# The last batch's attention ordered by query halves in a two-layer transformer kernel

## The chip, the cores and the metric

The kernel runs on one core of one Trainium2 chip. The metric is the device time of one execution in microseconds (us); every time below is in us unless it says ns. Engine names follow the profile: PE is the matmul engine and PEld its weight loads, DVE the vector engine, ACT the scalar (activation) engine, POOL the GpSimd engine, SP the sync engine, whose queue issues most of the DMAs.

## What is computed

Two transformer layers over a float32 tensor x of 4 batches, 1024 tokens each, 128 channels. Every sublayer is a layer norm with a per-batch scale and shift, the sublayer, and a gated addition to x. Cut to what matters here:

```python
# layer 0: causal attention, then a top-2 mixture of 8 experts (gelu)
# layer 1, attention
dense  = softmax(q @ k.T / sqrt(8)) @ v          # 16 heads of width 8
sparse = keep_top(softmax(Q @ K.T / 8), 204) ... @ V  # one head of width 64, renormalised
fused  = sig * (dense @ out_proj) + (1 - sig) * sparse
y = layernorm(h + fused) * g1 + b1
y = layernorm(y + relu(y @ ff1) @ ff2) * g2 + b2
x = x + gate * y
# layer 1, experts: top 2 of 8, at most 160 places for each expert and batch
h = layernorm(x) * (1 + cb) + sb
x = x + gate * (weighted sum of the two experts' relu MLPs)
```

## The kernel before

**Layout.** Tokens lie on the 128 partitions, 8 tiles of 128 tokens for each batch; "half h" means 4 tiles, or 512 tokens. The whole of x stays on the chip.

**Layer 1's attention loop.** The loop goes over units (batch b, head group g of 4 heads, query half h), 32 in all, and in each over 8 steps k (a tile of 128 keys). One step is written as two half-steps. A half-step computes scores for two heads (`weighed`: matmul `pw` from `kg` and `qa`, exponent `prT` on ACT), runs one piece of the row maxima for a later unit (`maxima`: two matmuls `pm` from `qg` and `kg`, one reduction `mxh` on DVE, twenty pieces ahead), and multiplies the previous step's exponents with the values (`values`: `pav`). At a unit's end its `pav` is copied to `raw`, transposed (`pr`) and divided into `cn` (`divided`). Before, a batch's units go through g, and for each g through both halves. `project(b, g)` loads q and k of a head group from DRAM (`qk`) by 8 DMAs on SP, into one of two `qg` and two `kg` buffers.

**Work beside the steps.** Everything else is written as generators (`Part`) that give up control after each piece and tell what it costs on P, A, D, G (PE, ACT, DVE, POOL). After each half-step, `between(n)` picks pieces whose due time has come, by a cost model of the four engines, which fixes the order in which each engine gets its instructions; each engine then runs its own list in order. A part has a first and a last step between which its work should be spread. The parts are:

- `begin(b)`: norm, q, k, v and the sparse head's projections of batch b
- `looked(b, four)`: the sparse attention of four query tiles; scores `pk`, exponents `exq`, a search for the threshold of the top 204 (ACT sign counts `junk`, DVE), exact selection (`lfq`, DVE), then `ended` for each tile: transposes `ptk` and the product `po` into `sp`
- `end(b)`: needs `cn` and `sp`; output projection (`ctxT`, `pdn`), norm l1, feed-forward in four blocks of 256 tokens (`ph`, `hid`, `pf`), norm l2, gated addition to x. Its additions and multiplications by rows run on POOL (`by_gpsimd`)
- `sends_of(b)`, through `sent_out`: norm f, transposes `ptf`, router (`pl`, `routed`, with the places `pp` from sums over all tokens before), and 16 indirect DMAs on POOL that scatter the tokens into the experts' places in DRAM (`sent`)

**The tail.** When the loop is over, its buffers are given up and `feed_forward` loads layer 1's expert weights (16 DMAs of 256 KB) into their room. `drain` then writes the rest, taking the first part in its list that the model says can start: the last batch's end and sends, `worked_on` for each batch in turn (per expert: `got` loaded, transposes `ptg`, `hs` on DVE, `ph`, `hid` on ACT, `py`, addition `y` on DVE, store to `done`), and `fetched` for each batch (16 indirect DMAs on POOL that gather `ys` from `done`, ACT and DVE work on them, and the store of the output). A batch's `worked_on` comes after the one before; the last batch's comes after its sends, and its gathers come last.

Layer 0 has the same parts at the start: two rounds of `worked_on`, the second of them beside the gathers of the first and the begin of layer 1's batch 0.

Of the kernel before, what the change touches and what calls it, by code (L numbers as in the profile page):

```python
# [15 lines left out]
P = 128  # L16
# [5 lines left out]
G = 4  # L22
# [21 lines left out]
TAX_A, TAX_D = (0.4, 3), (1.5, 2)  # L44
ROWS = ["out_b", "vp_b", "ff2_b", "ln1_g", "ln1_b", "ln2_g", "ln2_b"]
# [3 lines left out]
def kernel(ctx: ExitStack, tc: tile.TileContext, a: dict, out: bass.AP):  # L49
# [239 lines left out]
    def normalized(dst, src, name):  # L289

        n = src.shape[1]
        st = small.tile([P, n, 6], F32, tag="ln_st", name=f"st_{name}")
        mv = small.tile([P, n, 2], F32, tag="ln_mv", name=f"mv_{name}")
# [162 lines left out]
    def normal(dst, src, name):  # L456

        kind = name[:2].replace("0", "1")
        mv = small.tile([P, NT, 2], F32, tag=f"mv_{kind}", name=f"mv_{name}")
        bn = small.tile([P, NT, 6], F32, tag=f"st_{kind}", name=f"st_{name}")  # L460
        for i in range(NT):
            nc.vector.bn_stats(bn[:, i, :], src[:, i, :])
            if i % 4 == 3:
                yield "D!", ("D", 1.1)
        for i in range(NT):
            nc.vector.bn_aggr(mv[:, i, :], bn[:, i, :])
        rs = small.tile([P, NT], F32, tag=f"rs_{kind}", name=f"rs_{name}")
        nc.vector.tensor_scalar_add(rs, mv[:, :, 1], EPS)  # L468
        nc.gpsimd.tensor_tensor(rs, rs, mhalf, ALU.pow)  # L469
        yield "A", ("D", 1.4), ("G", 1.65)  # L470
        nb = small.tile([P, NT], F32, tag=f"nb_{kind}", name=f"nb_{name}")
        nc.vector.scalar_tensor_tensor(nb, mv[:, :, 0], -1.0, rs, ALU.mult, ALU.mult)
        for i in range(NT):
            nc.scalar.activation(
                dst[:, i, :], src[:, i, :], AF.Identity, bias=nb[:, i : i + 1],
                scale=rs[:, i : i + 1],
            )
            if i % 4 == 3:
                yield "A", ("D", 0.2 if i < 4 else 0.0), ("A", 1.15)

    def by_gpsimd(op, t, r):

        for h in range(NH):
            op(t[:, fours(h), :], t[:, fours(h), :], r(h))
# [19 lines left out]
    def routed(l, b, hT, wgt, wgtT, pool, ps, places=None):  # L504

        pl = ps.tile([P, NT, E], F32, tag="ms", name=f"pl{l}{b}")
        for i in range(NT):
            nc.tensor.matmul(
                pl[:, i, :], lhsT=hT[:, i * P : (i + 1) * P], rhs=router[l], start=True, stop=True
            )  # L510

        def new(tag, shape):
            return pool.tile(shape, F32, tag=tag, name=f"{tag}_{l}{b}")

        def wide(v):
            return v.unsqueeze(2).to_broadcast([P, NT, E])

        yield "D", ("P", 1.7)
# [13 lines left out]
        for i in range(NT):  # L532
            nc.vector.max(top[:, i, :], key[:, i, 0:E])
        yield "D", ("D", 1.5)
        nc.vector.memset(top[:, :, 2:8], KEY_PAD)
        left = new("r_left", [P, NT, 14])
        for i in range(NT):
            nc.vector.match_replace(left[:, i, :], top[:, i, :], key[:, i, :], KEY_CHOSEN)
        yield "D", ("D", 1.6)
# [16 lines left out]
        if l == 1 or places is not None:  # L556

            before = new("r_before", [P, NT, E])
            if l == 0 and b % 2:
                nc.vector.tensor_copy(before[:, 0, :], so_far[b - 1])  # L560
            else:
                nc.vector.memset(before[:, 0, :], 0.0)
            for i in range(1, NT):
                nc.vector.tensor_add(before[:, i, :], before[:, i - 1, :], chosen[:, i - 1, :])
            if l == 0 and b % 2 == 0:
                so_far[b] = new("r_so_far", [P, E])
                nc.vector.tensor_add(so_far[b], before[:, NT - 1, :], chosen[:, NT - 1, :])
            yield "", ("D", 1.4)
            pp = ps.tile([P, NT, E], F32, tag="ms", name=f"pp{b}")
# [8 lines left out]
        if places is not None:  # L578
# [5 lines left out]
                lg, pp, base[l].unsqueeze(1).to_broadcast([P, NT, E]), ALU.add  # L584
# [128 lines left out]
    def sent_out(l, b, xn, turn, fp):  # L713

        yield from normal(xn, x[:, b], f"f{l}")
# [9 lines left out]
        for h in range(NH):  # L725
# [11 lines left out]
            yield "!" if h == 0 else "", ("P", 1.1), ("A", 0.7)  # L737
        wgt = fp.tile([P, NT, E], F32, tag="wgt", name=f"wgt{l}{b}")
        into = fp.tile([P, NT, 2], mybir.dt.int32, tag="into", name=f"into{l}{b}", bufs=2)
        outof = const.tile([P, NT, 2], mybir.dt.int32, name=f"outof{l}{b}")  # L740
        both = const.tile([P, NT, 2], F32, name=f"both{l}{b}")
        yield from routed(l, b, hT, wgt, None, fp, ps, (into, outof, both))
# [3 lines left out]
        for i in range(NT):  # L746
# [14 lines left out]
        told[l, b] = outof, both  # L761

    def worked_on(l, q, w1, w2, b2r, act, fp):
# [63 lines left out]
        for i in range(len(units) + 2):  # L827
# [13 lines left out]
            if 1 <= i <= len(units):  # L841
                u = units[i - 1]
                for k0 in range(0, NK, 2):
                    up(u, k0)
                    us = u[2] * p / 512.0
                    yield "A!" if k0 == 0 else "!", ("P", 2.1 * us), ("A", 0.45 + 0.75 * us)
            if i >= 2:
                u = units[i - 2]
                down(u)
                yield "!", ("P", 1.07 * u[2]), ("D", 0.15 + 0.13 * u[2])  # L850
# [34 lines left out]
    def feed_forward(end, send):  # L885

        with tc.tile_pool(name="w1", bufs=1) as wpool, tc.tile_pool(name="f1", bufs=2) as fp:
# [11 lines left out]
            works[B - 1].after.append(send)  # L899
            drain([end, send, works[B - 1], gets[B - 1], *gets[:-1], *works[:-1]])  # L900
# [163 lines left out]
    def attention(general):  # L1064


        with tc.tile_pool(name=f"a1{general}", bufs=1) as ap, ExitStack() as wp_ctx:
# [19 lines left out]
            def turned(dst, src):  # L1087
                for h in range(NH):
# [4 lines left out]
                    yield "!" if h == 0 else "", ("P", 1.1), ("A", 0.6)  # L1093
# [3 lines left out]
            kgs = [ap.tile([P, T], F32, name=f"kg{i}") for i in range(2)]  # L1097
            for i in range(2):
                nc.gpsimd.memset(qgs[i], 0.0)
                nc.gpsimd.tensor_copy(kgs[i], ninth.to_broadcast([P, T]))  # L1100
# [26 lines left out]
            def project(b, g):  # L1127

                yield until(begins[b], "near", b)
                if g >= 2:  # L1130
                    assert ("qk", g - 1) in st[b]
                qg, kg = qgs[g % 2], kgs[g % 2]
                for s, to in ((1, kg), (0, qg)):
                    for j in range(4):
                        n = (4 * g + j) * DH
                        nc.sync.dma_start(
                            out=to[32 * j : 32 * j + DH, :], in_=qk[b][s, n : n + DH, :]
                        )
                st[b]["qk", g] = qg, kg
# [331 lines left out]
            def need(b, g):  # L1471

                if ("qk", g) not in st[b]:
                    projects[b, g].finish()
                return st[b]["qk", g]

            def shifted(b, g, h, mx):
# [5 lines left out]
                for q in range(4):  # L1483
# [5 lines left out]
                    qa, pt.rearrange("p q t -> p (q t)"), need(b, g)[0][:, half(h)], ALU.add  # L1489
# [4 lines left out]
            def maxima(b, g, h):  # L1494
# [3 lines left out]
                qg, kg = need(b, g)  # L1498
# [20 lines left out]
            def weighed(b, g, h, k, j):  # L1519
# [4 lines left out]
                    pw, lhsT=st[b]["qk", g][1][js, k * P : (k + 1) * P],  # L1524
# [4 lines left out]
            def values(b, g, h, k, part):  # L1529
# [20 lines left out]
                if (k, part) == (NT - 1, 1):  # L1550
                    raw = wp.tile([P, 512], F32, name="raw")
# [21 lines left out]
            def end(b):  # L1573
# [3 lines left out]
                by_gpsimd(nc.gpsimd.tensor_add, h_, lambda _: rows_of(o_b, 4))  # L1577
                by_gpsimd(nc.gpsimd.tensor_add, sp, lambda h: h_[:, fours(h), :])
                yield "!", ("G", 5.0)
                if b and not general:  # L1580
                    yield over(sends[b - 1])
                ctxT = ap.tile([P, T], F32, tag="x1T", name="ctxT")
                yield from turned(ctxT, cn)
                for h in range(NH):
# [9 lines left out]
                    yield "!" if h == 0 else "D", ("P", 1.1), ("D", 0.8)  # L1594
                x1 = h_
                yield from normal(x1, sp, f"l1{b}")
                for op, n in ((nc.gpsimd.tensor_mul, "ln1_g"), (nc.gpsimd.tensor_add, "ln1_b")):
                    by_gpsimd(op, x1, lambda _: rows_of(row[n], 4))
                    yield "", ("G", 2.5)
                x1T = ap.tile([P, T], F32, tag="x1T", name="x1T")  # L1600
                yield from turned(x1T, x1)
                by_gpsimd(nc.gpsimd.tensor_add, x1, lambda _: rows_of(row["ff2_b"], 4))
                spend(("G", 2.5))
                for q in range(4):
# [23 lines left out]
                    yield "!" if q < 3 else "D", ("P", 1.8), ("D", 0.45)  # L1628
                yield from normal(sp, x1, f"l2{b}")
                for t in (row["ln2_g"], row["ln2_b"], brow1[:, b, 0, :]):  # L1630
                    op = nc.gpsimd.tensor_add if t is row["ln2_b"] else nc.gpsimd.tensor_mul
                    by_gpsimd(op, sp, lambda _: rows_of(t, 4))
                    yield "", ("G", 2.5)
                by_gpsimd(nc.gpsimd.tensor_add, x[:, b], lambda h: sp[:, fours(h), :])
                yield "", ("G", 2.5)
# [224 lines left out]
```

## Time and profile before

| | us |
|---|---|
| three runs: lowest, median, highest | 1981.0, 1983.44, 1988.71 |
| the profiled execution, its own time | 1983.17 |
| its span in the profile | 1981.4 |
| start of layer 1's loop (first `pav`) | 439.5 |
| start of the last batch's units (first `pav` of unit 25 of 32) | 1447.1 |
| end of the loop (last `pav`) | 1767.9 |
| PE's work for the last batch's experts ends | 1935.2 |

PE shows 1759.9 of busy time, DVE 1285.4, ACT 1146.1, POOL 511.1. A stretch's busy share must be read against what else could run in it: in the loop, PE's busy time counts matmuls that overlap, and in the tail the four engines wait for each other and for DMAs. From 1935.2 to the end PE does next to nothing; the chain there is gathers and their use.

### The profile page before, as it was taken

To read this page: it belongs to the slowest core of one execution; us is meant where nothing else is said; L and a number is where in the kernel's file an instruction comes from. 1 tells how busy PE (TensorE), PEld (TensorE's weight loads), DVE (VectorE), ACT (ScalarE), POOL (GpSimd) and SP (SyncE) were. 2 spreads that over 40 slices of the span, in tenths; PEclk is the share of its full clock that TensorE was granted. 3 is DMA by queue.
4 is the path that set the end of the run, shared out by engine and by line. 5 is a ranking of instruction groups with operands and counts; after the bars stand their busy time and mean duration, and the time that the engine had idled before them with its cause. 6 is when DMAs were issued, how large, how long until landed. Compare 5 with 4: busy or idle time off the path is not lost. (4 is left out here: it accounts for less than half of the span.)

```text
span 1981.4 us, 33712 instructions
## 1 busy us (share of the span) xinstructions
PE 1759.9 (89%) x12801; PEld 910.4 (46%) x12801; DVE 1285.4 (65%) x3135; ACT 1146.1 (58%) x2316; POOL 511.1 (26%) x531
## 2 busy tenths in 40 slices
PE   6885998899999999998999999999999999969970
PEld 5654776452333434423443443344434325338870
DVE  4665414547887786478888658878765799622423
ACT  3533434136877755686865578686458976645331
POOL 1043445123111020112232012214201022324644
PEclk9997998899999999998999999999999999999885
DMA  8201332110000000000000000000000000021333
GB/s 291 83 33 42 91 86 83 38 48 23 13 17 12 7 6 2 6 1 17 12 20 1 6 7 1 17 12 20 3 5 6 1 6 1 14 90 45 82 71 60
DMA packets 75291, 68.40 MB, mean 35 GB/s; under 512 B 13237, under 2 KB 64774, under 8 KB 75120
## 3 DMA queue, kind: packets, MB, share of 16 engines
q1 hardware_dynamic: 66496, 50.59, 8.2%
q0 software_dynamic: 8192, 15.16, 3.4%
q8 instruction: 103, 1.69, 0.4%
q14 instruction: 68, 0.56, 0.1%
q10 hardware_dynamic: 432, 0.40, 0.1%
HBM read 35.24 MB, written 32.51 MB: 34 GB/s over the span
## 5 line engine op out<-in xcount | busy, mean ns | idle before, releaser
L1511 DVE TENSOR_REDUCE mxh<-pm 128x2 f32<-128x1024 f32 x512 | 619.8, 1219 | 207.3 <-PE pm L1507 204.6
L1523 PE MATMUL pw<-qa,kg 32*128 32x512 f32 x2048 | 701.0, 652 | 42.0 <-ACT prT L1527 30.7
L1527 ACT ACTIVATE prT<-pw 128x512 f32<-128x512 f32 x1024 | 556.7, 596 | 290.8 <-PE pm L1507 175.5
L1507 PE MATMUL pm<-kg,qg 32*128 32x512 f32 x2048 | 590.9, 657 | 7.5 <-DMA qg<-qk 5.4
L1523 PEld LDWEIGHTS pw<-qa,kg 32*128 32x128 f32 x2048 | 216.6, 186 | 308.0 <-issue 148.6
L1545 PE MATMUL pav<-prT,v_more 128*9 128x256 f32 x3584 | 283.7, 389 | 0.0
L1545 PEld LDWEIGHTS pav<-prT,v_more 128*9 128x9 f32 x3584 | 53.6, 88 | 349.1 <-issue 348.1
L806 ACT ACTIVATE hid<-ph,b 128x160 f32<-128x160 f32 (+2 forms) x256 | 100.6, 458 | 189.9 <-PE ph L801 189.6
L1378 ACT ACTIVATE junk<-exq,now 128x1024 bf16<-128x1024 f32 x160 | 185.0, 1156 | 9.3 <-DVE now L1405 8.5
L861 POOL DMA_INDIRECT ys<-done,outof x128 | 129.1, 1009 | 207.4 <-DMA qg<-qk 73.7
L1461 POOL TENSOR_TENSOR exq<-exq,lfq 128x512 f32<-128x512 f32 x64 | 81.0, 1288 | 341.8 <-DVE lfq L1459 323.7
L1507 PEld LDWEIGHTS pm<-kg,qg 32*128 32x128 f32 x2048 | 158.7, 187 | 20.6 <-issue 7.1
L801 PE MATMUL ph<-hs,w 128*128 128x160 f32 (+2 forms) x512 | 132.2, 402 | 9.6 <-DVE mxh L1511 4.4
L816 PE MATMUL py<-w,hid 128*128 128x128 f32 (+1 forms) x1152 | 139.5, 277 | 0.0
L816 PEld LDWEIGHTS py<-w,hid 128*128 128x128 f32 (+1 forms) x1152 | 136.0, 175 | 6.7 <-issue 3.0
L801 PEld LDWEIGHTS ph<-hs,w 128*128 128x128 f32 x512 | 90.4, 210 | 34.0 <-DVE mxh L1511 9.2
L821 DVE TENSOR_TENSOR y<-py,b2r 128x384 f32<-128x384 f32 (+1 forms) x64 | 29.1, 455 | 105.3 <-PE py L816 105.1
L748 POOL DMA_INDIRECT sent<-xns,into x64 | 63.3, 989 | 76.6 <-DVE into L600 28.4
L469 POOL TENSOR_TENSOR rs_l<-rs_l,mhalf 128x8 f32<-128x8 f32 x8 | 13.2, 1652 | 256.0 <-DVE rs_l L468 256.0
L1311 PEld LDWEIGHTS po<-sV,exT 128*128 128x128 f32 x512 | 60.9, 194 | 15.8 <-issue 7.7
L1311 PE MATMUL po<-sV,exT 128*128 128x129 f32 x512 | 67.2, 285 | 0.3 <-ACT exT L1307 0.3
L973 ACT ACTIVATE pr<-pscr,nm 128x128 f32<-128x128 f32 (+7 forms) x32 | 23.6, 739 | 70.0 <-DVE nm L970 36.2
(513 smaller groups left out, 2191.2 us busy)
## 6 DMA issues: line engine op xcount, KB each, us to landing
w<-in_w_dram SPq DMA_DIRECT2D x32, 256.0 KB
sent<-zero SPq DMA_DIRECT2D x2, 2560.0 KB
qk<-near SPq DMA_DIRECT2D x8, 512.0 KB
got<-sent SPq DMA_DIRECT2D x16, 192.0 KB
done<-y SPq DMA_DIRECT2D x16, 192.0 KB
sent<-zero SPq DMA_DIRECT2D x4, 640.0 KB
got<-sent SPq DMA_DIRECT2D x32, 80.0 KB
done<-y SPq DMA_DIRECT2D x32, 80.0 KB
```

What stands on the lines that cost most here:

```text
L801: nc.tensor.matmul(ph[:, k - k0, : m * p], lhsT=w1[:, e, k * P : (k + 1) * P], rhs=hss[u][:, : m * p], start=True, stop=True,)
L806: nc.scalar.activation(hids[u][:, k, : m * p], ph[:, k - k0, : m * p], act, bias=b1[l][:, e * NK + k : e * NK + k + 1],)
L816: nc.tensor.matmul(py[:p, i, :], lhsT=hids[u][:, k, i * p : (i + 1) * p], rhs=w2[:, e, k, :], start=(k == 0), stop=(k == NK - 1),)
L861: nc.gpsimd.indirect_dma_start(out=y, out_offset=None, in_=done[l][of(l, b)][:], in_offset=bass.IndirectOffsetOnAxis(ap=outof[:, i, k : k ...
L1311: nc.tensor.matmul(po, lhsT=exT[:, k, :], rhs=sVs[b % 2][:, k, :], start=(k == 0), stop=(k == NT - 1),)
L1378: nc.scalar.activation(junk, ex, AF.Sign, bias=now[:, i, 0:1], scale=-1.0, accum_out=now[:, i, 1:2],)
L1461: nc.gpsimd.tensor_tensor(ex[:, half(h)], ex[:, half(h)], lf[:, half(h)], ALU.subtract)
L1507: nc.tensor.matmul(pm[:, jj, :], lhsT=qg[js, t0 : t0 + P], rhs=kg[js, half(kh)], start=True, stop=True,)
L1511: nc.vector.tensor_reduce(mx[:, q, j0 : j0 + 2, kh], pm, AX.X, ALU.max)
L1523: nc.tensor.matmul(pw, lhsT=st[b]["qk", g][1][js, k * P : (k + 1) * P], rhs=qas[b, g, h][js, :], start=True, stop=True,)
L1527: nc.scalar.activation(prs[b, g, h, k][:, j, :], pw, AF.Exp)
L1545: nc.tensor.matmul(to, lhsT=v, rhs=pr[:, j, cs], start=(k == 0), stop=((k, part) == (NT - 1, 1)),)
```

## The change

For the last batch only, the units go through query half 0 for all four head groups, then half 1. Its `end` and `sends` become two parts each, one for each half. The parts of half 0 wait for the first `looked` part of that batch, and are due between steps 38 and 54 of its 64 steps; those of half 1 come after the loop. The running sums of the router's places pass from half 0 to half 1 (`so_far`). q and k are now loaded for each of the eight units (k whole, q by half), with a third `kg` buffer. Due times of the second last batch's end and sends and of the last batch's two `looked` parts are changed (`LAST`); the statistics' buffers and `raw` have one buffer in place of two. In `worked_on`, the cost constants that the order is planned by go from 2.1 to 1.8 and from 1.07 to 0.9, which also moves instructions in layer 0.

```diff
+LAST = (18, 20, 30, -3, 33, 7, 60, 38, 50, 54)
...
-    def normal(dst, src, name):
+    def normal(dst, src, name, hs=(0, 1)):
...
-        for i in range(NT):
+        its = [4 * h + k for h in hs for k in range(4)]
+        for i in its:
             nc.vector.bn_stats(bn[:, i, :], src[:, i, :])
...
-    def routed(l, b, hT, wgt, wgtT, pool, ps, places=None):
+    def routed(l, b, hT, wgt, wgtT, pool, ps, places=None, hs=(0, 1)):
+        n = 4 * len(hs)
+        behind = l == 0 and b % 2 or hs == (1,)
+        before_more = l == 0 and b % 2 == 0 or hs == (0,)
...
-                    yield "A!" if k0 == 0 else "!", ("P", 2.1 * us), ("A", 0.45 + 0.75 * us)
+                    yield "A!" if k0 == 0 else "!", ("P", 1.8 * us), ("A", 0.45 + 0.75 * us)
...
-                yield "!", ("P", 1.07 * u[2]), ("D", 0.15 + 0.13 * u[2])
+                yield "!", ("P", 0.9 * u[2]), ("D", 0.15 + 0.13 * u[2])
...
-            drain([end, send, works[B - 1], gets[B - 1], *gets[:-1], *works[:-1]])
+            drain([*rest, works[B - 1], gets[B - 1], *gets[:-1], *works[:-1]])
...
+            def turn_of(b, g, h):
+                return 4 * h + g if b == last else g
...
+                g = u % 4
+                if b == last:
+                    qg, kg, cs = qgs[u % 2], kgs[(0, 2, 1)[u % 3]], half(u // 4)
+                else:
+                    qg, kg, cs = qgs[u % 2], kgs[u % 2], slice(0, T)
+                for s, to, cs in ((1, kg, slice(0, T)), (0, qg, cs)):
...
-            def end(b):
+            def end(b, hs=(0, 1)):
...
             units = [(b, g, h) for b in range(B) for g in range(G) for h in range(NH)]
+            if last:
+                units[8 * last :] = [(last, g, h) for h in range(NH) for g in range(G)]
...
+                if b == last:
+                    for h in range(NH):
+                        to, so, on = (n + k for k in (LAST[7:] if h == 0 else (per + 0.5, per + 12, per + 25)))
+                        ends[b, h] = Part(end_of_half(b, h), 36.0, to, so)
+                        sends[b, h] = Part(
+                            sends_of_half(b, h), 26.0, so, on, [ends[b, h]]
+                        )
+                    for u in range(1, 8):
+                        to = n + 8 * u - 13
+                        projects[b, u] = Part(project(b, u), 1.0, to, to + 1)
...
-                        Part(looked(b, 0), 106.0, n + 1, n + 33),
-                        Part(looked(b, 1), 106.0, n + 6, n + 58),
+                        Part(looked(b, 0), 106.0, n + LAST[3], n + LAST[4]),
+                        Part(looked(b, 1), 106.0, n + LAST[5], n + LAST[6]),
...
+                    if b == last:
+                        ends[b, f].after = [part]
...
-                    feed_forward(ends[B - 1], sends[B - 1])
+                    feed_forward([ends[last, 0], sends[last, 0], ends[last, 1], sends[last, 1]])
```

## The prediction

> **What bounds the kernel now.** I read the page first, then the table of busy time by stretch for the last batch's eight units (a unit is one head group and one query half, eight steps; its start is its first `pav` from `v_first`) and the tail, then each engine's timeline in the tail, and the chain that ended last.
>
> ```profile
> span 1981.4 us, 33712 instructions
> PE 1759.9 (89%) x12801; PEld 910.4 (46%) x12801; DVE 1285.4 (65%) x3135; ACT 1146.1 (58%) x2316; POOL 511.1 (26%) x531
> ```
> ```profile
> 1478.80:1542.00 63.20, 57.35 (x391) 26.66 (x388) 36.31 (x69) 51.08 (x105) 7.56 (x6) 0.97 0.02 5
> 1542.00:1579.40 37.40, 36.09 (x263) 11.82 (x260) 30.46 (x82) 33.46 (x65) 3.64 (x4) 1.00 0.01 1
> 1579.40:1618.90 39.50, 36.44 (x262) 11.47 (x259) 38.27 (x63) 29.82 (x58) 13.79 (x13) 0.91 0.03 7
> 1696.60:1726.10 29.50, 29.38 (x235) 9.54 (x232) 20.90 (x54) 17.80 (x33) 12.52 (x12) 1.00 0.06 18
> 1726.10:1767.90 41.80, 38.31 (x274) 20.44 (x272) 6.85 (x18) 19.50 (x36) 13.20 (x13) 0.96 0.01 4
> 1767.90:1792.20 24.30, 12.25 (x70) 10.33 (x70) 4.91 (x23) 8.14 (x18) 9.13 (x7) 0.79 0.65 209
> 1792.20:1825.90 33.70, 33.41 (x273) 32.53 (x271) 11.99 (x54) 18.67 (x56) 13.20 (x10) 1.00 0.10 28
> 1825.90:1867.20 41.30, 34.19 (x237) 33.31 (x237) 19.01 (x93) 15.74 (x47) 23.38 (x23) 0.82 0.33 81
> 1867.20:1907.80 40.60, 29.01 (x209) 28.17 (x209) 15.25 (x46) 13.45 (x42) 25.26 (x25) 0.84 0.41 84
> 1907.80:1935.20 27.40, 27.33 (x208) 26.61 (x208) 6.03 (x16) 11.37 (x36) 7.99 (x8) 0.89 0.21 59
> 1935.20:1981.40 46.20, 0.19 (x2) 0.12 (x2) 15.37 (x52) 4.81 (x12) 24.26 (x24) 0.52 0.40 61
> ```
> The columns are stretch, length, then busy time of PE, PEld, DVE, ACT, POOL, then clock. The loop ends at 1767.9; 213.5 us of tail follow: the last batch's end and sends (feed-forward, router, scatter), four batches of expert work of which the fourth, clean, takes 27.4, and 46.2 for the last gathers. In the loop "PE busy" misleads: a unit with nothing beside it lasts 28.7, because `pw` and `pm` run together in different rows of the array; yet the third line, with no side work on PE at all, lasts 39.5. DVE is full there (38.27). The 63.2 unit has ACT at 51.08. So the loop is held by PE in some units and by DVE or ACT in others.
>
> ```profile
> 1903.50 0.35 DVE L874 SCALAR_TENSOR_TENSOR ys<-ys,both,ys 128x128 f32<-128x128 f32 x1 [2.09 <-DMA ys<-done,outof]
> 1904.42 0.41 DVE L821 TENSOR_TENSOR y<-py,b2r 80x256 f32<-80x256 f32 x1
> ```
> ```profile
> 1905.77 1.88 DMA got<-sent
> 1907.78 1.00 PE ptg L791 x4
> 1908.82 2.50 PE ph L801 x8
> ...
> 1915.64 1.13 PE ph L801 x8
> ```
> ```profile
> 324.98 1.11 PE L1091 MATMUL pt<-ident,h__2997 128*128 128x128 f32 x4 [4.51 <-POOL h__2997 L484]
> ```
> The third batch's last `y` had its `py` at 1899.1 but stands behind a gather's use on DVE until 1904.4, so the next batch's loads and PE come late. The last line, in layer 0, is a PE pause that the changed cost constants touch.
>
> **The change part by part.** I use the emitted order of both kernels (the changed one built, not run) and durations of the trace.
>
> *PE moved from tail to loop.* Half an end and half the sends: two turns and a `ptf`, 3 x 0.55; `pdn` 0.95; two feed-forward blocks, 2 x (1.75 + 1.8) = 7.1; `pl` 0.85; one more `pp` pair 0.4: 10.9 us, at full clock. With it go some 12 us of DVE, 6 of ACT, 8 additions and multiplications by POOL at 1.26, three `pow`, and 8 scatters at 1.3.
>
> *The loop.* For each unit of the last batch I sum PE (28.3 plus side work), DVE and ACT from these durations and take the largest. Before, the seven units to 1726.1: 275 against 279 measured, so the method holds to 1.5%. After: the first look begins earlier (units of ACT 58.7 + 40.6 become 56.7 + 38.1), the fifth rises from 40.3 to 44.8 (DVE; the previous batch's sends and four tiles' transposes fall together), the seventh from 29.4 to 47.8 (PE: the half's feed-forward and six `po` tiles): 291, plus 16. The last unit loses three of its four `po` tiles' work: 12.7 less 3.3, minus 9.4. Sum +6.5; with some stalls +7 (between +3, if DVE's and ACT's slack takes more, and +13, all of PE's share and 2 of stalls).
>
> *Tail to the first expert batch's end.* Before 58.0 after loop end. After, for half as many tiles: `pdn`'s use ends at +5.2, statistics to 6.5, `pow` 8.2, four ACT 10.2, POOL multiply and add 12.8 (before 15.5), the two blocks to 24.1. Then DVE's order puts l2's `nb`, which waits for POOL's `pow`, ahead of `hs`: experts start at 28.4, where 24.3 was usual. The sends' chain (POOL 5.0, `pow`, ACT) is ready near 40, the router follows, and 8 units of 3.02 end near 58.8: minus 0.8 saved. The cover that the moved blocks gave is gone: the chain binds, not PE.
>
> *Here the clock counts.* The row: after a pause of 3.08 before the second batch, and of 8.64 before 1907.78, `ph` takes 2.50 and 2.16 before returning to 1.13, with `ptg` 1.00 instead of 0.14: about 3 us. [...] I take the row; it speaks against the change.
>
> *Second to fourth batch.* Before: starts at +0, +38.2, +78.8, end +106.2 from the second's start, plus 3.1 of pause. After, no router beside the second (27.4), but its last `y` stands on DVE behind the eighth pair of gathers. POOL does 8 scatters and 16 gathers at 1.3: two scatters come before the stores land (+2.9), the rest ends at +31.5; landing and use put the `y` at 35.3, the third start at 38.4 (before 41.3). The third: its gathers, free of scatters, end at about 27 after that `y`, `hs` of its last unit waits 2 to 3: 32.7 (before 40.6). The fourth 27.4. From the first batch's end: 98.5 against 109.3, minus 10.8. Three pauses remain. With the 0.8 lost, the tail gives minus 10 (between minus 16, gathers landing in 2.7 us and no clock loss, and minus 4, in 4.8 and twice late).
>
> *The last 46.2.* Eight gathers of the third batch and 16 of the fourth still follow the last `y` in DVE's order: unchanged.
>
> *Layer 0.* The constants 1.8 and 0.9 place two more `ph` (1.4) and eight `py` (1.9) ahead of the `pt` that waits 4.51. PE then pauses 1.3, and the slow `ph` and `pvh` behind it (2.9 too long) stay fast. Minus 4 (0 to minus 7).
>
> *Priced at nothing.* The third key buffer's fill is 1.03 on POOL, inside an 18 us pause there (cost 1 without it). The last batch's 32 extra q and k loads: SP issues at 0.36 to 0.5 each, at most 16 us, on a queue that holds nothing else until the weights, with two steps or more before use; PE waited 5.4 for such loads in the whole run, so between 0 and 5; I take 0. Single buffers for statistics are written and read by DVE in order; `raw` is reused a unit (29 us) later. `pow` on four columns lies between half of 1.65 and 1.65; I take 1.65. The other DVE pieces on 4 tiles cost what 8 cost (0.17 to 0.22), which is in the sum.
>
> *Sum* against the profiled execution, 1983.17 (span 1981.4 and 1.8 around it): +7 - 10 - 4 = -7, so 1976. That execution is 0.3 under the median of the runs, 1983.44.
>
> **The rivals.** About 0.5%, 9.9 us, is what a measurement of this kernel tells from no change.
>
> *The full gain.* Delays by gathers vanish and the loop absorbs the half: +3 - 16 - 5 = -18, 1965. For it: DVE has 2.38 of 28 us busy near the loop's end, and each late `y` is a matter of 2 us. Against: emitted DVE order still has all of gets before the last `y`.
>
> *Slower: the first half's scatters slip past the loop.* In POOL's order the 8 scatters (10.4) and two additions (2.5) stand ahead of the second half's `pow`, which is wanted 6.6 after loop end. If `into` comes later than 6 before loop end, each us is one of tail. The emitted order gives it in the last unit, some 18 before loop end: about 12 to spare. Late by 24 beyond that point, it costs -7 + 24 = +17, 2000; from 17 late it is measurably slower. Against: `pp` is 12 half-steps of 1.8 before the end.
>
> *It doesn't do what it says.* If the first half ended only at the loop's end, its 10.9 would return to the tail: about 1981. The emitted order has its feed-forward among the steps of the seventh unit, so this is nearly out.
>
> **How the numbers follow.** Within 0.5%, around the sum: 0.5, its own range 1973.5 to 1986. The full gain, or a good part of it beyond 9.9: 0.35. Slower by more: 0.15, of which half is stalls in the crowded seventh unit or a slipped POOL queue. The parts at their ends give -27 and +9 together, rarely all at once; for 8 in 10 I take 1962 to 1993.
>
> **What would show it.** Right: loop end (last `pav`) 3 to 13 later than 1767.9 less what layer 0 gave; first `pav` of the run 3 to 6 before 439.5; experts' first `ptg` at +24 with `hs` at +28; fourth batch's end at about +157 after loop end, not +167; 46 for the rest. Wrong: the seventh unit well over 50, `pl` of the first half after the last `pav`, a third-batch start less than 35 after the first batch's end, or layer 0's loop start unmoved.

## The result: slower by 0.7%, and the profile after

The changed kernel took 1999.01 us (median of 5 runs, 1991.27 to 2003.35) where the kernel before took 1983.44 (5 runs, 1980.89 to 1989.67): a ratio of 1.0072, 95% interval 1.005 to 1.0095. The forecast was 1976, between 1962 and 1993. The profiled execution took 1999.01, its span is 1997.1, so 15.7 longer than before's span. From the head of the page of the changed kernel:

```profile
PE 1771.8 (89%) x12805; PEld 915.8 (46%) x12805; DVE 1280.0 (64%) x3168; ACT 1145.2 (57%) x2317; POOL 511.2 (26%) x535
```

PE has 11.9 more of busy time for four more matmuls: the same work ran at a lower granted clock (0.939 over the span, 0.945 before), or with less overlap. The table of busy time by stretch says where. Columns as before: stretch, length, PE, PEld, DVE, ACT, POOL, clock. A stretch is one unit, counted from 0 over the whole loop. Units 14, 22 and 28 of the kernel before:

```profile
1025.70:1062.00 36.30, 35.98 (x315) 14.69 (x313) 34.10 (x53) 18.43 (x34) 9.36 (x11) 1.00 0.01 2
1364.20:1404.00 39.80, 38.64 (x311) 15.59 (x308) 30.56 (x51) 18.39 (x35) 11.76 (x12) 0.96 0.01 2
1618.90:1656.10 37.20, 36.18 (x295) 14.38 (x292) 35.64 (x83) 26.43 (x49) 7.71 (x7) 1.00 0.01 2
```

The same three and unit 30 of the changed kernel (unit 30 of before is the 29.50 of the prediction's table):

```profile
1013.50:1060.30 46.80, 44.60 (x327) 19.34 (x324) 31.77 (x55) 18.30 (x34) 14.09 (x15) 0.85 0.02 4
1362.00:1407.80 45.80, 44.73 (x315) 18.78 (x313) 30.73 (x51) 18.38 (x34) 11.76 (x12) 0.81 0.01 3
1624.50:1675.70 51.20, 48.35 (x380) 24.95 (x376) 42.08 (x141) 35.65 (x69) 16.50 (x16) 0.97 0.05 15
1706.90:1760.90 54.00, 50.71 (x372) 26.63 (x368) 29.55 (x86) 31.12 (x63) 16.90 (x14) 1.00 0.00 1
```

Units 14 and 22 lie in the second and third batch, where nothing had been expected. Unit 14 took 36.3 before and 46.8 now, unit 22 took 39.8 and now 45.8, both at a clock far below 1.00. Units 28 and 30 are the fifth and seventh of the last batch: 37.2 and 29.5 before, 51.2 and 54.0 now. The last unit and the tail in the same view:

```profile
1760.90:1789.20 28.30, 28.15 (x202) 10.56 (x200) 4.92 (x31) 15.70 (x30) 10.42 (x10) 1.00 0.06 19
1789.20:1814.60 25.40, 14.71 (x68) 12.22 (x69) 3.21 (x14) 6.70 (x15) 4.83 (x4) 0.66 0.68 199
1951.00:1997.00 46.00, 0.19 (x2) 0.11 (x2) 15.08 (x52) 4.82 (x12) 24.13 (x24) 0.52 0.38 61
```

The loop's last unit is 28.3 instead of 41.8, the loop ends at 1789.2, the experts' first product comes 25.4 later, and the last gathers take their 46 again. Summed by stage, from the starts of the units (before, after, difference; the loop is counted here to the start of its last `pav`, 0.4 before that `pav` ends):

| stage | before | after | difference | forecast |
|---|---|---|---|---|
| until the first `pav` | 439.5 | 427.3 | -12.2 | -4 |
| batches 0, 1, 2 | 315.5, 351.1, 341.0 | 314.7, 361.3, 348.1 | +16.5 | 0 |
| last batch, to its last `pav` | 320.4 | 337.4 | +17.0 | +7 |
| tail | 213.9 | 208.3 | -5.6 | -10 |
| span | 1981.4 | 1997.1 | +15.7 | -7 |

Every row differs from its forecast, the second by the most. These are two single executions, though. A later run, `e18`, has TensorE's order of before up to the last batch, and its three batches took 320.4, 355.0 and 346.5: 14.3 more than before's in sum. So only a part of the second row can be the change's; the experiments say which.

### The profile page after: what moved, and what is told of

Its sections match the earlier page's. It is cut to its first block, busy times and chain, and to the rows that moved or that the text cites. A ratio compares the mean times of both kernels' runs of the same rounds, so it can differ in the third digit from the quotient of the medians.

```text
span 1997.1 us, 33809 instructions
## 1 busy us (share of the span) xinstructions
PE 1771.8 (89%) x12805; PEld 915.8 (46%) x12805; DVE 1280.0 (64%) x3168; ACT 1145.2 (57%) x2317; POOL 511.2 (26%) x535
## 4 chain that ended last, share of the span: by engine, by line
PE 68%; DVE 13%; ACT 10%; issue 3%; DMA 3%; POOL 2%; SPq 0%; DVEq 0%; ACTq 0%; POOLq 0%
PE pw L1547 25%; PE pav L1569 11%; PE py L826 5%; PE ph L811 5%; DVE mxh L1535 3%; PE po L1334 3%; PE pm L1531 2%; ACT prT L1551 2%; DMA ys<-done,outof 2%; ACT junk L1401 2%; DVE nm L1307 2%; PE pf L1646 2%; PE pk L1302 2%; ACT exq L1310 2%; PE ph L1633 1%
## 5 line engine op out<-in xcount | busy, mean ns | idle before, releaser
L1531 PEld LDWEIGHTS pm<-kg,qg 32*128 32x128 f32 x2048 | 159.6, 187 | 13.5 <-DVE mxh L1535 5.7
L826 PE MATMUL py<-w,hid 128*128 128x128 f32 (+1 forms) x1152 | 141.7, 280 | 0.0
L811 PEld LDWEIGHTS ph<-hs,w 128*128 128x128 f32 x512 | 88.8, 207 | 36.3 <-DVE mxh L1535 7.9
L472 POOL TENSOR_TENSOR rs_l<-rs_l,mhalf 128x8 f32<-128x8 f32 (+1 forms) x10 | 14.0, 1401 | 239.3 <-DVE rs_l L471 239.3
```

The costliest lines, as they stand in the source:

```text
L811: nc.tensor.matmul(ph[:, k - k0, : m * p], lhsT=w1[:, e, k * P : (k + 1) * P], rhs=hss[u][:, : m * p], start=True, stop=True,)
L826: nc.tensor.matmul(py[:p, i, :], lhsT=hids[u][:, k, i * p : (i + 1) * p], rhs=w2[:, e, k, :], start=(k == 0), stop=(k == NK - 1),)
L1531: nc.tensor.matmul(pm[:, jj, :], lhsT=qg[js, t0 : t0 + P], rhs=kg[js, half(kh)], start=True, stop=True,)
```

## The experiments

The time of a kernel is given as a ratio to the kernel before on the same chip. There were two kinds of chip: on some, before took 1983 to 1987 (here called steady), on others 2079 to 2095 (stalling; the last section says what stalled). The parts were tried on both, since the halves cost more on the stalling ones.

### The planner's rounded figures

The emitted orders of both kernels differ in units 13 to 15, long before the last batch. The planner's prices are the costs that a piece tells the cost model; they are no part of the computation. The change writes the planner's price of the router's running counts as 0.17 per tile; for eight tiles that is 1.36 instead of 1.4. This alone, put into the kernel before (run `e1`), moves one `po` tile out of unit 13 into unit 14:

```
-            yield "", ("D", 1.4)
+            yield "", ("D", 1.36)
```

> The kernel before with one number changed: the planner's price of the router's running counts, 1.4, becomes 1.36, as the changed kernel has it for eight tiles. No instruction is added or removed; in the emitted order the fourth `po` tile of the third batch's query tile moves from unit 13 to unit 14, and the chain `pkn`, `pg`, `pu`, `pe` behind it. Theory A (this order is what cost unit 14 of the changed kernel its 10.5 us, 36.3 to 46.8): about 1983 + 10 = 1993, unit 14 at 44 to 47. Theory B (the lost time of batches 1 and 2 is chance of the clock's windows and comes and goes from run to run): 1983, unit 14 near 38 with at most one half-clock window more.

Measured, on a stalling chip: 1.0017 (1.0004 to 1.003). Unit 14 took 48.1. The reverse, in the changed kernel (`e2`):

```
-            yield "", ("D", 0.17 * n)
+            yield "", ("D", 0.175 * n)
(and 0.175, 0.2125, 0.1875 per tile for the other three)
```

> The changed kernel with the planner's prices of `normal` and `routed` written so that they give the old values exactly for eight tiles (0.175, 0.2125, 0.1875, 0.175 per tile); nothing else. Theory A: unit 14 goes back to about 36 and the time to 1999 - 10 = 1989. Theory B: 1999 as it is.

Measured on the same chip: 1.005 (1.0032 to 1.0068), and unit 14 was back at 36.3. So the order does cause the long unit, but the whole of `e1` was 3.6 slower, not 10. Repeated twice (`e9`, `e13`):

> Again the kernel before with the one planner price 1.4 as 1.36. On the other chip it cost 3.6 us (0.4 to 3.0 thousandths), where units 13 and 14 together took 105.7 against 97.4 in the kernels with the old number. Theory A (unit 14's bunched chain costs 10 us wherever bursts of scatters do not stall VectorE and ScalarE beside it): unit 14 at 46 to 47, 0.4 to 0.5% slower than before. Rival (it is worth 3 to 4 us, and the rest of batch 1's loss has another source): 0.2%, unit 14 near 42.

> The one planner price 1.4 as 1.36 in the kernel before, a third time. Theory A (without stalls beside scatters it costs what units 13 to 15 of the changed kernel lost, 9 to 10 us): 0.4 to 0.5% slower. Rival (it is worth 3 us everywhere): 0.15%.

Both on stalling chips: 1.0011 (0.9999 to 1.0024) and 1.0002 (0.998 to 1.0024). Unit 14 was 47.0 and 46.9, but unit 13, where scatters stall the other engines on such chips, was 57.1 in both instead of 60 to 61: a part of the cost went under in a stall. By these three the figure costs about 2 us on such a chip, less than theory A's 10 each time. Units 13 to 15 together took 147.0 to 148.7 with the moved `po` there and 141.2 to 141.7 without, so a part of their 5 to 7 came back elsewhere; where was not found. What the figure costs on a steady chip was seen last, with the changed kernel (`e16`) beside itself with the old figures (`e17`):

> The changed kernel, unedited. Where scatters do not stall the other engines: +0.5 to +0.8% as twice before. Where they do: theory A (parts add up: old figures' +0.5%, the figures' 0.1%) +0.6%; rival (the figures cost 10 us on top of the halves) +1.0%.

> The changed kernel with the old price figures of `normal` and `routed`, so that units 13 to 15 are placed as before. Theory A (the bunched chain of unit 14 costs the 9 to 10 us by which batch 1 is longer): without stalls 0 to +0.2%; with stalls +0.5% as before. Rival (batch 1's loss is mostly given back elsewhere): within 3 us of the changed kernel.

1.0077 (1.0054 to 1.0101) and 1.0031 (1.0007 to 1.0055): 0.0046 of 1984, or 9 us. These two intervals touch, and the two profiled executions do not settle it: with the rounded figures it was the fastest of its ten runs (1990.85), with the old ones the slowest of its twelve (2002.03). What can be compared is the place where the orders differ. Batch 1 took 361.9 with the rounded figures and 352.5 with the old ones, and unit 14 with the old ones was:

```profile
1019.20:1055.40 36.20, 35.88 (x311) 14.64 (x308) 34.01 (x53) 18.37 (x34) 9.33 (x10) 1.00 0.01 2
```

Over all twenty profiles, unit 14 took 46.8 to 48.1 in the seven with the `po` in it and 36.2 to 37.7 in the thirteen without. On steady chips units 13 to 15 together took 132.6 against 123.9 to 125.3, so the order costs 7 to 9 us there.

Why one tile costs so much, the timeline of the changed kernel shows (start, duration, engine, what it waited for):

```profile
1016.12 2.06 PE L1334 MATMUL po<-sV,exT 128*128 128x129 f32 x16
...
1033.00 2.00 PE L1239 MATMUL pkn<-two_w,hT 128*128 128x64 f32 x16
...
1034.31 2.48 POOL L1484 TENSOR_TENSOR exq<-exq,lfq 128x512 f32<-128x512 f32 x2
...
1036.89 1.15 PE L1251 MATMUL pg<-kn 128*64 128x65 f32 x16 [1.90 <-POOL kn L1246]
...
1038.35 3.78 PE L1263 MATMUL pu<-sQ,gram 64*128 64x512 f32 x4 [0.31 <-DVE gram L1255]
...
1042.06 3.57 PE L1273 MATMUL pe<-weigh,prod 128*128 128x3 f32 x16
```

The same two products in the kernel before:

```profile
1034.64 1.98 PE L1240 MATMUL pu<-sQ,gram 64*128 64x512 f32 x4
...
1038.54 1.95 PE L1250 MATMUL pe<-weigh,prod 128*128 128x3 f32 x16
```

The displaced `po` makes the next batch's guess (`pkn`, `pg`, `pu`, `pe`) late, and the planner then issues these four at a stretch, with no step between them to cover the way over ScalarE, POOL and VectorE; before, steps of `pw`, `pm` and `pav` stood between each two of them. `pg` waits 1.90 because a small memset on POOL stands behind a product of 2.48. From 1038.4 to 1052.0 the granted clock is 0.50: `pu` takes 3.78 and `pe` 3.57, where before took 1.98 and 1.95. As an estimate from these rows, the `po` itself is 2.1 of unit 14's 10.5, the two pauses 2.2, and half of the 13.7 at half speed 6.8. The clock fell in this unit in all seven profiles with this order (its mean is 0.85 in the changed kernel's three and in `e9`); whether the pauses or the narrow products bring that about was not tested. Unit 22 has the same order in both kernels, with the chain bunched, and there the clock varies: it took 41.3 at 0.92 and 45.8 at 0.81 in profiles of the changed kernel, and 39.7 to 45.6 in versions of the kernel before. So unit 14's 10.5 belongs to the order, and unit 22's 6.0 need not be the change's at all.

### The halves, without the rest

Here the changed kernel got the old prices everywhere (`e4`, `e10`, `e14`, `e18` in this order). TensorE's order up to the last batch is then that of the kernel before.

> The changed kernel with the old prices everywhere (2.1, 1.07, and those of `normal` and `routed`): what stays is the last batch by halves with its due times, and up to the last batch the order of TensorE is that of the kernel before. Theory A: loop +17 in the last batch, tail -6, so 1983 + 11 = 1994. As the prediction had it: +7 - 10, 1980. Rival (the last batch's loss is also clock): 1984 to 1988.

> Again the changed kernel with the old planner prices everywhere. On the other chip it was 1.25% slower than before. Theory A (additive: after's +10 on this chip is layer 0's -12, the one number's +8 and the halves' rest): 0.6 to 0.8% slower, last batch's loop 337 to 339 against 320, tail 207 to 210 against 214. Rival (the halves cost 26 us here too, and something else in the changed kernel gives it back): 1.2%.

> The halves alone, a third time. Theory A (the halves cost 26 to 30 only where scatters stall the other engines; where not, loop +18 and tail -5): 0.6 to 0.8% slower. Rival (26 us or more here too, given back in the changed kernel by layer 0's order and more): 1.2 to 1.5%. If this chip stalls again, the last batch's loop is near 368 and nothing new is told.

> The halves with the old prices everywhere. Theory A: without stalls +0.6 to +0.8%; with them +1.2 to +1.5% as three times before. Rival: +1.2% or more without stalls too.

Measured: 1.0125 (1.0098 to 1.0151), 1.0146 (1.0112 to 1.018) and 1.0119 (1.0089 to 1.0148) on stalling chips, 1.0088 (1.0062 to 1.0113) on a steady one. On no chip was the splitting worth its price: where the prediction had -3 for it (+7 in the loop, -10 in the tail), the steady chip gave +17.5 (0.0088 of 1984, interval 12 to 22). By the three kernels that ran together there, the changed kernel's +15.3 (0.0077) splits into the halves, +17.5, the expert prices, -11.3 (1.0031 less 1.0088), and the figures, +9.1; the last two, as differences of ratios with such intervals, are uncertain by some 7 each.

The changed kernel itself, once more on a steady chip (`e5`):

> The changed kernel once more, unedited, as the base for the others on the same chip. Theory A (the sum of its parts is a property of the order): +0.5 to +1.0% of the kernel before on this chip too, loop of the last batch 15 or more us longer than before's 320, tail 4 to 8 shorter. Rival (its loss is chance of the clock's windows): within 0.3% of before.

1.0049 (1.0028 to 1.0069); batches 315.7, 360.2, 347.8, 338.3 and tail 208.9, each within 1.1 of the first profile. Beside it the moved half was put back behind the loop (`e6`):

```
-LAST = (18, 20, 30, -3, 33, 7, 60, 38, 50, 54)
+LAST = (18, 20, 30, -3, 33, 7, 60, 64.5, 76, 89)
```

> The changed kernel with three due times changed, 38, 50, 54 to 64.5, 76, 89: the first half's end and sends go back behind the loop; the units stay by halves. Theory A (the moved half is paid in full in the loop and saves little in the tail): loop of the last batch 15 to 20 us shorter than in the changed kernel, tail 10 to 16 longer, sum -5. As the prediction had it (the half's 10.9 of TensorE returns to the tail, the loop gives back the same): loop -11, tail +11, 0.

Measured: 1.0084 (1.0059 to 1.0109), so slower than the changed kernel, against theory A's sum. The loop's part of that theory held: 319.1 against 338.3, 19 shorter. Its seventh unit:

```profile
1700.40:1737.80 37.40, 36.43 (x291) 15.82 (x288) 22.07 (x42) 21.14 (x39) 8.72 (x7) 1.00 0.01 1
```

That is 37.4, against 55.1 in the changed kernel on the same chip. TensorE's time in both, divided by the trace's records, with time in which two overlap counted once: side products take 21.3 against 8.9, `pw` and `pm` a further 22.6 against 19.9, `pav` 8.1 against 7.7, and nothing runs for 3.1 against 1.0. So 12.4 of side work cost 17.7. About 1 of that is the clock (the unit took 54.0 at 1.00 in the first profile of the changed kernel); the rest is pauses, 2.1 more, most of which end with ScalarE's or POOL's results, and `pw` running alone for longer. The pairs in which `pw` and `pm` run beside each other are not lost: they run at once for 10.6 in `e6` and for 10.6 in that first profile. The fifth unit is not the moved half's: it took 48.8 here too.

The tail's part failed: 238.8 against 208.9. One line of TensorE's timeline has most of it:

```profile
1940.73 1.05 PE L801 MATMUL ptg<-ident,got 80*128 80x80 f32 x4 [25.45 <-DMA got<-sent]
```

In this order the second half's router stood among the uses of gathers on VectorE, and its scatters stood on POOL behind sixteen gathers (1905.9 to 1926.9), so the fourth batch's experts waited 25.45 for them. What the two halves cost in a tail without that pause was not measured.

### The expert blocks' prices

First the new prices alone, in the kernel before (`e3`):

> The kernel before with only the expert blocks' planned prices changed, 2.1 to 1.8 and 1.07 to 0.9. Theory A (layer 0 gains what the changed kernel's trace shows, loop start 439.5 to 427.3): 1983 - 12 = 1971. As the prediction had it: -4, 1979. Rival (the early start is given back by the clock later): 1983.

0.9954 (0.9938 to 0.997) on a stalling chip. The loop began at 457.1, where the kernels with the old prices on that chip had 474.6 and 482.1, but the tail took 243.8, 9 more than the 234.9 of `e1`: in the emitted order, five more pairs of gathers had slipped behind the last `y`. So the price was changed in layer 0 alone (`e7`):

```
-("P", 2.1 * us)
+("P", (2.1 if l else 1.8) * us)
(and 1.07 to 0.9 in the same way)
```

> The kernel before with the planned prices of the expert blocks at 1.8 and 0.9 in layer 0 alone, the old ones in layer 1, so that the tail's order is that of before. Theory A (layer 0 gains 12 to 17, and it was the tail's changed order that took 9 of it away where the prices changed everywhere): 0.6 to 0.8% faster than before. Rival (later clock windows give it back): 0.3% or less. As the prediction had it: 4 us, 0.2%.

0.9936 (0.9916 to 0.9957) on a steady chip: 12.7 us, with none of the halves. Over all steady profiles the loop began at 421.7 to 428.8 with the new prices, at 439.5 and 432.7 with the old, so 4 to 18 us earlier. The view of waits, TensorE in layer 0 (engine, line, awaited: sum, times, longest), in the kernel before:

```profile
PE pm L1507 <- DMA qg<-qk: 5.4, 1, 5.4
PE pt L1091 <- POOL h__2997 L484: 4.5, 1, 4.5
```

And the same view of the changed kernel:

```profile
PE pt L1101 <- POOL h__3015 L487: 3.3, 2, 2.7
PE pm L1531 <- DMA qg<-qk: 2.6, 1, 2.6
```

The `pt` that the prediction priced gained 1.2, the wait for the first q and k loads 2.8, and all of TensorE's waits from 300 us to the loop together fall from 21.0 to 13.9. The rest of the 12 I did not assign. A part is chance: the half-speed stretch at the kernel's very start (eight `prm` take 2.08 in it and 1.13 behind it, with 1.00 in the clock column) ended at 29.4 before and at 24.6 after, and over the steady profiles it ends between 23.8 and 29.9 with the old prices as with the new. On the steady chip above, the new prices (in both layers) gave 11.3 inside the changed kernel.

### The gathers of the tail

On top of layer 0's new prices (`e8`):

> As the one with layer 0's prices, and the list handed to the planner behind the loop names the gathers ahead of the last batch's experts, so that the third batch's eight pairs of gathers lie beside the fourth batch's expert work instead of behind it. Theory A: fourth batch 27 to 33, the stretch behind it 46 to 25, so 15 us less than with layer 0's prices alone: 1.2 to 1.5% faster than before. Rival (the gathers' uses on VectorE make each `hs` and `y` late, as in the third batch, and the fourth batch takes 45): no gain over layer 0's prices alone.

```
-drain([end, send, works[B - 1], gets[B - 1], *gets[:-1], *works[:-1]])
+drain([end, send, *gets[:-1], works[B - 1], gets[B - 1], *works[:-1]])
```

0.9936 (0.9913 to 0.9959), no better than layer 0's prices without it: the rival was right. The stretch behind the last `y` fell from 46.4 to 37.6, but that `y` came 10.0 later after the loop's end (174.6 instead of 164.6). VectorE's timeline in `e8`'s fourth batch:

```profile
1909.80 0.35 DVE L874 SCALAR_TENSOR_TENSOR ys<-ys,both,ys 128x128 f32<-128x128 f32 x1 [2.01 <-DMA ys<-done,outof]
...
1913.51 0.35 DVE L874 SCALAR_TENSOR_TENSOR ys<-ys,both,ys 128x128 f32<-128x128 f32 x1 [2.30 <-DMA ys<-done,outof]
...
1917.50 0.41 DVE L821 TENSOR_TENSOR y<-py,b2r 80x256 f32<-80x256 f32 x1
```

Each use waits for its gather, and `y` and `hs` wait behind the uses. The planner prices a pair of gathers at 2.1 and the trace at 2.6, so it orders each use too early. With the price corrected in layer 1 (`e11` with 2.6, `e12` and `e15` with 3.0):

```
-spend(("G", 2.1))
+spend(("G", 2.6 if l else 2.1))
...
-yield "DG!", ("-", 2.1), ...
+yield "DG!", ("-", 2.6 if l else 2.1), ...
```

> The kernel with layer 0's prices and the gathers named ahead of the last experts, and in layer 1 the planned price of a pair of gathers at 2.6, what the trace shows (two at 1.0 and 0.3 between), instead of 2.1. Theory A (it was the late uses on VectorE that spoilt the fourth batch: with the price right, the use is placed when the gather has landed): fourth batch 30 down to 23 to 25, third batch's late y earlier by 3 to 5, 1.0 to 1.2% faster than before. Rival (POOL's rate binds: 32 pairs at 2.6 are 83 us whatever the order): 0.6%, as without it.

> As the one with the price 2.6, with 3.0: each use stands still later in VectorE's order, and two more pairs of gathers go behind the last y. Theory A: fourth batch 22 to 24 and the stretch behind it 5 to 8 longer than with 2.6, so within 3 us of it. Rival (landing, 2 to 3 us behind the issue, still makes uses late at 2.6): 5 us or more faster than with 2.6.

> Layer 0's prices, the gathers ahead of the last experts, and the gathers' price 3.0, once more. Theory A (12 of its gain are layer 0's, 9 the tail's order): 0.9 to 1.2% faster than before, tail 202 to 206 against 214. Rival (the tail's gain came from the stalls of the other chip): 0.6%.

All three met stalling chips: 0.9936 (0.9912 to 0.996) with 2.6, and 0.9898 (0.9872 to 0.9925) and 0.9889 (0.9865 to 0.9912) with 3.0. The right price for issuing alone gave nothing more. With 3.0 it was 8 us less on the same chip, as `e12`'s rival said, though the two intervals just touch. That the landing is the reason is not shown: with 2.6 VectorE's waits for landings are already down to 0.8 before the experts end (19.9 in the kernel with 2.1 on the steady chip), and stalls of 18 and more lie beside them. With 3.0 the tail took 221.9 and 223.9, against 229 to 235 with before's tail order on such chips. This is the best version found, 21 to 23 us faster than before there and without the halves; on a steady chip it did not run.

## Why the prediction was wrong

In short: the steps that failed are the halves' cost in the loop, mis-sized (+7, measured +17), and a step that was missing, the rounded figures (nothing, about +9). Layer 0's gain was also mis-sized, and the tail's by less. The rounded figures alone don't make the sign: with the old ones the changed kernel was still 1.0031 (1.0007 to 1.0055).

*Layer 0 (-4, measured -12).* The direction was right, the mechanism only in part. I priced the one wait that I had shown, from 4.51 to 1.3; it gained 1.2. I took the q and k loads' wait of 5.4 as given; it halved. Most of the 12 is neither, and its cause stays open.

*Batches 0 to 2 (nothing, measured +16.5).* This step was missing; 8.7 of it is the order of units 13 to 15, the rest lies within what the same order shows between two profiles. I read the diff's `0.17 * len(its)` and `0.17 * n` as the old figures for eight tiles, and compared the emitted orders only where the change was meant to act. A `po` of 2.06 that goes from unit 13 to unit 14 leaves their sum for TensorE the same, and a sum by engine can't see that a dependent chain has lost its cover.

*The last batch (+7, measured +17).* Five of the seven unit sums nearly held: the first to fourth and the sixth, 198.4 in all (291 less the other two), took 37.0, 59.6, 37.8, 38.7 and 31.2, so 204.3. The two that carry over 16 us of side products failed: 44.8 became 51.2, and 47.8 became 54.0. I had the fifth held by VectorE; in its 51.2 VectorE was busy for 42.1 and TensorE for 48.4. For the seventh I added the side products to a base of 28.3, as if TensorE would never wait; its 54.0 holds 1.5 more of side products than the 19.5 that I had counted, 3.3 of pauses (before's seventh unit has 0.1), and 1.5 more of the steps themselves. The line that I had named as a wrong sign, the seventh unit well over 50, came true. The last unit gave back 13.5, more than the 9.4 forecast. What I had priced at nothing (third key buffer, extra loads, single buffers) cost nothing in sum: with all of it and the units' new order, but without the moved half, the loop took 319.1, before 320.4.

*The tail (-10, measured -5.6).* Up to the first batch's end every point was met: experts' `hs` at +28.6 (28.4), batch end at +58.6 (58.8). The third start, 39.5 from there, was forecast at 38.4. The term that failed is the third batch: 36.7 against 32.7. The timeline of the changed kernel:

```profile
1907.89 1.33 PE L811 MATMUL ph<-hs,w 128*128 128x160 f32 x8 [1.23 <-DVE hs L844]
...
1910.18 0.35 DVE L884 SCALAR_TENSOR_TENSOR ys<-ys,both,ys 128x128 f32<-128x128 f32 x1 [2.43 <-DMA ys<-done,outof]
...
1914.39 1.32 PE L811 MATMUL ph<-hs,w 128*128 128x160 f32 x8 [3.42 <-DVE hs L844]
```

I had the wait on `hs` at 2 to 3 once; it came twice, 1.23 and 3.42, some 2 of the 4.0. The rest is not assigned; the pause of 3.14 before the fourth batch is one of the three that the forecast had. The last 46.2 stayed, as forecast.

*The rivals.* The first half's scatters did not slip: they ended at 1784.0, and POOL waited 10.06 for VectorE before the second half's `pow` at 1796.69, near the 12 that I had to spare. The change did what it says.

*The clock.* The row that I took for pauses (3.0) gave 58.8 for the first batch's end; 58.6 was measured. That alone does not show the 3.0: the pause that the change added was 3.21 (at 1818.27), the granted clock was 0.51 from 1820.0 to 1823.4, and the eight `ph` at 1820.15 took 2.50 and the sixteen `py` behind them 2.41, where the next ones took 1.29 and 1.91; as an estimate from these rows that cost 1.2 and 0.5. The row does not cover half-speed stretches inside the loop either: unit 14's 13.7 at 0.50 alone cost some 6.8.

*The range.* The parts at their lower ends sum to -20 (+3, -16, -7), not to the -27 that I wrote; at their upper ends +9, as written. The loop's term alone left its range of +3 to +13.

## What to carry to other kernels

Work moved from a tail that waits into a loop whose TensorE is full pays its full price there and more (here 17.7 for 12.4), and frees in the tail only what stands on the chain. A planner's figure is code: a rounding of 0.04 us moved one tile, and the units around it took 7 to 9 us more on a steady chip, so compare the emitted order everywhere, and look for dependent chains that have lost the work between their links. A use that was ordered before its transfer had landed held up everything behind it in its engine's queue (in `e8` the two uses shown waited 2.01 and 2.30 for their gathers, with `hs` and `y` behind them).

## What the hardware did that was not expected

*The clock fell without a pause.* In the changed kernel with the old figures (`e17`), TensorE's timeline at the end of the last batch:

```profile
1748.87 0.60 PE L736 MATMUL ptf<-ident,h__11123 128*128 128x128 f32 x4
...
1751.72 1.06 PE L516 MATMUL pl<-router,hTf 128*128 128x8 f32 x8
1752.64 0.64 PE L1329 MATMUL ptk<-ident,exq 128*128 128x128 f32 x4
1753.20 2.19 PE L1547 MATMUL pw<-qa,kg 32*128 32x512 f32 x4
...
1774.57 1.13 PE L1547 MATMUL pw<-qa,kg 32*128 32x512 f32 x4
```

From 1753.2 to 1774.6 the products took up to twice their time (`pw` 2.08 to 2.26 instead of 1.13), and in the 18 us before it no row shows a pause over 0.25. The last unit took 34.5 (to 1792.8) at a clock of 0.77 there, and 28.3 at 1.00 in the first profile of the changed kernel. TensorE's order in this unit and the one ahead of it is the same in all five steady profiles that have the moved half in the loop; the clock fell at this place in two of them (this one, for 21.4 by the rows, and `e18`, where a `pav` from `v_first` took 1.06 at the last unit's start and 0.59 to 0.62 at most others) and not in the other three. Pauses went with most falls: in the loop of the changed kernel's first profile the clock fell to 0.50 sixteen times, and the longest pause in the 10 us before was 0.8 to 2.8 fourteen times, 4.2 once and under 0.1 once. In both places (here and unit 14) narrow products or products without a partner lie at the fall: here `pl`, 8 columns wide (eight in 1.06), and `pw` on 32 rows with no `pm` beside it (four in 1.84), there `pe`, 3 columns wide (sixteen in 3.57). That this is the cause was not tested. The spread of the runs goes with the clock: those of this kernel went from 1979.4 at a mean clock of 0.949 to 2002.0 at 0.939.

*On some chips VectorE and ScalarE stalled beside bursts of scatters and gathers.* The longest of ScalarE's waits of this kind in `e3`, where before took 2094.9:

```profile
ACT hid L806 <- remote: 32.9, 6, 10.4
```

The releaser `remote` stands for something that the profile does not hold. In all, ScalarE has 60.6 of it and VectorE 95.3 in this run, and neither has any in the nine profiles of steady chips. Three rows of unit 13 there:

```profile
1039.93 0.97 POOL L748 DMA_INDIRECT sent<-h__3013,into  x1 [0.30 <-issue]
1040.99 0.16 DVE L1316 SCALAR_TENSOR_TENSOR ro<-zq,po 128x1 f32<-128x1 f32 x1 [6.61 <-remote]
1041.03 0.60 ACT L1527 ACTIVATE prT<-pw 128x512 f32<-128x512 f32 x1 [5.76 <-remote]
```

POOL goes on issuing scatters while the others stand still. Unit 13 takes 61.2 there against 43.6. Each stall of over 1.5 us in `e3` lies beside indirect DMAs of POOL. With the halves another half burst of scatters lies inside the loop, and its last batch took 358 to 370 instead of 329. What delays the engines, and why on some chips only, stays open; each chip was used in one stretch of time, so it could also be the time and not the chip.
